# Two graph layers with residual norms on one core: when the norm steps of a pair enter the instruction streams

## The chip, the cores and the metric

The kernel runs on one core of a Trainium2 chip. The core's engines work side by side, each through its own stream of instructions in a fixed order: TensorE (PE in the profile) multiplies matrices and writes to PSUM, VectorE (DVE) and ScalarE (ACT) do elementwise work and read PSUM out, GpSimd (POOL) does elementwise work on SBUF, and SyncE (SP) issues the transfers. Engines wait for each other by semaphores. The metric is the device time of one execution in microseconds, the median of several; lower is better.

## The reference

There are 64 graphs of 256 nodes with 512 features. Two layers follow each other, each with a residual and a layer norm:

```python
# layer 0
deg = sum(adj, axis=-1)
agg = (adj @ x) / max(deg, 1e-6)
x1  = layernorm(x + relu(concat([x, agg]) @ W.T))
# layer 1
q, k = split(x1 @ Wqk);  v = x1 @ Wv
agg  = adj @ (k * mask)
w    = mask * (q . agg) / sqrt(512)          # one score per node
out  = layernorm(x1 + softmax(w, over nodes) * v)
```

All is fp32. The kernel forms `Wq Wk^T` once, so that layer 1 needs one product of x1 for the scores, one for the values and one with adj.

## The kernel before

Graphs are handled in 32 pairs. Every large product is a block product of the Strassen kind: seven products P1 to P7 of sums of blocks instead of eight. P1, P2, P3 and P5 are split a second time by `inner`, P4, P6 and P7 are done by `outer`, and products with adj by `gather`. The sums of blocks are made ahead by VectorE and GpSimd.

`inner` works with a bank `w` and a pair of banks `q`. Each unit ends in copies by ScalarE that the next unit of the same product, or the next product on the same bank, must wait for:

```python
def inner(p, X, sides, w, q, done=lambda fifth: None):
    ...
    def first_two():
        mm(hi, s(0), b["T1"], start=True)
        mm(lo, X.chunk(block, 0, 0), b["B11"])
        act.copy(q[0][:, :HF], lo)
        tick()
    def second():
        mm(lo, s(1), b["T2"])
        act.copy(q[0][:, HF:], lo)
        tick()
    def third():
        mm(lo, s(2), b["T3"])
        act.copy(q[1]..., lo[...])                 # 512 columns
        act.copy(fifth[0], hi)
        mm(q[0][:, :HF], X.chunk(block, 0, 1), b["B21"])
        tick()
    def last_two():
        mm(q[1][:, :HF], X.chunk(block, 1, 1), b["T4"])
        mm(q[0][:, HF:], s(3), b["B22"])
        if p in ("P1", "P5"):
            for k in range(2):
                vec.tensor_add(q[k][:, HF:], q[k][:, HF:], fifth[0])
        done(fifth[0])                             # copies or adds the product out
        tick()
```

The program is written out by `run`, whose string names the order of the units; `run("i k i k", ...)` takes a unit of i, one of k, and so on. Work that belongs to no product (norms, softmax, masks, degrees) stands in `chains` and is taken step by step by `tick`, after a unit, when a clock kept while the program is built says that the step's engine would be free. `room` is how far ahead of that clock an engine may be booked (0.6 us; -9.0 lets it take nothing), and `flush` takes all steps of a chain at once:

```python
def tick():
    while not quiet[0]:
        for c in list(chains):
            if c[2][0] <= clock[0] and c[3][0][0].free <= clock[0] + room[c[3][0][0]]:
                step(c)
                break
        else:
            return

def hasten(name, left):
    for c in list(chains):
        if c[1] == name and len(c[3]) == left:
            step(c)
            step(c)
```

A norm of one graph (two tiles of 128 nodes, NT = 2) is this chain; its last scaling opens a further chain with the two transposes of the tiles (`turn`), and after those of both graphs 16 transfers place the transposed x1:

```python
return [(vec, mean)] + [(act, lambda t=t: square(t)) for t in range(n)] + [(act, factor), (vec, shifts)] + [
    (act, lambda t=t: scale(t)) for t in range(n)]
```

In the profile `square` is `junk<-own,less`, `factor` is `rstd`, `shifts` is `shift<-less,rstd`, and `scale` is `own<-own,shift,rstd`. `adj<-adj,mask_sb` are the masks of adj for layer 1.

The main loop, with the parts concerned (j is the pair; layer 0 of pair j is interleaved with layer 1 of pair j - 1):

```python
i = inner("P1", X, W0, pw[0], u, a1)
k = inner("P5", X, W0, pw[1], y, a5)
m = inner("P2", X, W0, pw[0], o, a2)
...
elif j == 1:
    early.append(a1)
    run("k i k m k i k", i=early[0], k=k, m=m)
    fourth_sums(X, [1])
    run("m p p", m=m, p=p)
...
else:                                     # j > 1
    run("i k", i=i, k=k)
    send_scores(j - 2)
    run("i l k", i=i, k=k, l=open1)
    flush("norm")
    ...
...
if j == 1:
    turn_here(Y, owns[0], 0, pw)          # transposes by TensorE, for the first pair
    flush("mask")
    sumsM[0] = adj_sums(0)
    load_rows(2)
    run("s", s=s)
    turn_here(Y, owns[0], 1, pw)
    inner_sums(Y, gp, 0)
    ...
# end of layer 1 of pair j - 1; p is its P4, open1 its P3
b8()
run("p l p l", p=p, l=open1)
if j < NP - 1:
    hasten("norm", NT + 1)
run("p l", p=p, l=open1)
```

Of the kernel before, what the change touches and what calls it, by code (L numbers as in the profile page):

```python
# [94 lines left out]
def resnorm_kernel(  # L95
# [15 lines left out]
    NT, NF, NA = N // P, F // P, A // P  # L111
    H, HF = NF // 2, F // 2
    NP = B // 2
# [21 lines left out]
    room = {vec: 0.6, act: 0.6}  # L135
# [8 lines left out]
    def step(chain):  # L144
        _, name, ready, steps = chain
        eng, work = steps.popleft()
        work()
        ready[0] = eng.free + (0.4 if eng is not vec else 0.7 if name == "norm" and len(steps) == NT else 2.2 if name == "finish" or name == "norm" and steady else 1.4) if steps and steps[0][0] is not eng else 0.0
        if not steps:
            chains.remove(chain)  # L150
# [10 lines left out]
    def flush(*names):  # L161
        while True:
# [1 line left out]
            if not c:  # L164
                return
            step(c)

    def hasten(name, left):

        for c in list(chains):  # L170
            if c[1] == name and len(c[3]) == left:
                step(c)
                step(c)

    def run(order, **units):
        for name in order.split():
            units[name].pop(0)()
# [454 lines left out]
    def turn_here(X, x1, k, ps):  # L632

        for t in range(NT):
            for c in range(NF):
                tc.keep_in_program_order(nc.tensor.matmul(
                    ps[t][:, c * P:(c + 1) * P], x1[:, k, t, c * P:(c + 1) * P], ident, is_transpose=True,
                    start=(c == 0), stop=True, skip_group_check=True))
            act.copy(X.a[:, k, :, :, t].rearrange("p h e m -> p (h e) m"), ps[t].rearrange("p (c m) -> p c m", c=NF))
# [123 lines left out]
    pu, py, pf, pw = banks  # L763
# [3 lines left out]
    for j in range(NP):  # L767
        X = Xs.pop(j)
        if j == 2:
            steady.append(True)  # L770
        flush("finish")
        owns[j] = pool.tile([P, 2, NT, F], F32, name="own", bufs=3)
        if j > 0:
            load_adj(j)
            run_now(late_sums)
            late_sums.clear()
            sumsA[j] = adj_sums(j)

        u, y, o = pf, py, pu
        ys[j] = pool.tile([P, 2, NT, F], F32, name="y")  # L780
        a1, a2, a3, a4, a5, a6, a7 = layer0(j, o, u, y)
# [3 lines that stand above are left out]
        p, q = pairs(u, X, S2, W0["T2"], a6), pairs(u, X, S3, W0["T3"], a7)  # L785
        r, s = inner("P3", X, W0, pw[1], y, a3), pairs(u, X, A22, W0["T4"], a4)
        if j == 0:
            run("i k i k i k i k", i=i, k=k)
            flush("degrees")
            load_rows(1)  # L790
        elif j == 1:
            early.append(a1)
            run("k i k m k i k", i=early[0], k=k, m=m)
            fourth_sums(X, [1])
            run("m p p", m=m, p=p)
            fourth_sums(X, [0])
            run("p p m", m=m, p=p)
            load_x(1)
# [5 lines that stand above are left out]
            fetch_scores(j - 2)  # L804
            places[0](range(16))
            run("i k i k", i=i, k=k)
        if j != 1:
            fourth_sums(X, [1])
        if j > 1:
            flush("mask")  # L810
            sumsM[j - 1] = adj_sums(j - 1)
            if j + 1 < NP:
                load_rows(j + 1)
            load_x(j)
        if j > 1:
            softmax(j - 2)
            shared[0] = 1.0
        if j != 1:
            run("m p p", m=m, p=p)
            fourth_sums(X, [0])  # L820
            run("m p p m", m=m, p=p)
        flush("w0a")
        run("q q q", q=q)
        flush("w0")
        run("r q r m", m=m, q=q, r=r)
        if j == 1:
            flush("norm")
        quiet[0] = j < 2
        room[vec] = -9.0 if j > 1 else 0.6
        run("r s r", r=r, s=s)  # L830
        if j > 0:
            Y = x1Ts.pop(j - 1)
        if j > 1:
            inner_sums(Y, gp, 0)
            queue(1, "sums", *outer_sums(Y, vec), (vec, lambda Y=Y: inner_sums(Y, gp, 1)))
        T_late = []
        T = sums_T(ys[j], T_late, 0 if j < 2 else 1)

        if j == 0:
            degrees(1)  # L840
        zs[j] = pool.tile([P, 2, NT, HF], F32, name="z")
        g = gather(sumsA.pop(j), T, zs[j], pw[1], y[1], y[0], owns[j], rdegs[j], T_late)

        def sums_next():
            if j == NP - 1:
                return
            inner_sums(Xs[j + 1], gp, 0)
            rest = outer_sums(Xs[j + 1], gp)
            run_now(rest[:1])
            inner_sums(Xs[j + 1], gp, 1)  # L850
            late_sums.extend(rest[1:])
        if j == 0:
            sums_next()
            held = [c for c in chains if c[1] == "w1"]
            chains[:] = [c for c in chains if c[1] != "w1"]
            early.append(inner("P1", Xs[1], W0, pw[0], u, lambda fifth: early[1](fifth)))
            run("s s a b s c d i e i g f", s=s, i=early[0], **g)
            quiet[0] = False
        else:
            u2, o2, y2 = o, pf, y  # L860
            b1, b2, b3, b4, b5, b6, b7, b8 = layer1(j - 1, ys[j][:, :, 0], o2, u2, y2)
            jj = inner("P1", Y, W1, pw[0], u2)
            k = inner("P2", Y, W1, y[0], o2, b2)
            if j == 1:
                turn_here(Y, owns[0], 0, pw)
                flush("mask")
                sumsM[0] = adj_sums(0)
                load_rows(2)
                run("s", s=s)
                turn_here(Y, owns[0], 1, pw)  # L870
                inner_sums(Y, gp, 0)
                sums_Y = (*outer_sums(Y, vec), (vec, lambda: inner_sums(Y, gp, 1)))
                run("s a b s d c", s=s, **g)
                quiet[0] = False
                flush("w1")
                run("e j g f", j=jj, **g)
                queue(1, "sums", *sums_Y)
                run("k j k j k j", j=jj, k=k)
                b1(None)
                run("k", k=k)  # L880
            else:
                run("s s j s a b", s=s, j=jj, k=k, **g)
                room[vec] = 0.6
                run("j", j=jj)
                if j < NP - 1:
                    degrees(j + 1)
                run("c d j k e j", s=s, j=jj, k=k, **g)
                quiet[0] = True
                run("k", k=k)
                quiet[0] = False  # L890
                b1(None)
                run("g f", **g)
        flush("softmax", "adds", "sums", "degrees")
        if j > 0:
            aggs[j - 1] = late.tile([P, 2 * N_SIDE], F32, name="agg").rearrange(
                "p (k t f) -> p k t f", k=2, t=NT)
            vs[j - 1] = [late.tile([P, NT, F], F32, name="v", bufs=2) for _ in range(2)]
            T = sums_T(owns[j - 1])
            g = gather(sumsM.pop(j - 1), T, aggs[j - 1], pw[0], o2[1], o2[0])
            h, q = pairs(u2, Y, S2, W1["T2"], b6), pairs(u2, Y, S3, W1["T3"], b7)  # L900
            n = inner("P5", Y, W1, pw[1], y2, b5)
            p, open1 = pairs(u2, Y, A22, W1["T4"], b4), inner("P3", Y, W1, pw[1], y2, b3)
            norm0(j)
            mask_adj(j)
            run("k h h" if j > 1 else "h h", k=k, h=h)
            if j == 1:
                degrees(2)
                flush("degrees")
            if j < NP - 1:
                load_xT(j + 1)  # L910
            run("n k h h" if j > 1 else "n h h", k=k, n=n, h=h)
            fourth_sums(Y)
            shared[0] = 1.25
            sums_next()
            run("a n b q d q n c q e q n p g f", n=n, q=q, p=p, **g)
            b8()
            run("p l p l", p=p, l=open1)
            if j < NP - 1:
                hasten("norm", NT + 1)
            run("p l", p=p, l=open1)  # L920
            py, pu = pu, py
        else:
            norm0(0)
            mask_adj(0)
            chains.extend(held)
# [113 lines left out]
```

## Time and profile before

| | before |
|---|---|
| median of 3 runs | 1907.98 us (1907.01 to 1908.05) |
| span of the profiled execution | 1906.3 us |
| TensorE, matmuls | 1862.3 us, 98% |
| VectorE | 1502.3 us, 79% |
| ScalarE | 1309.5 us, 69% |
| GpSimd | 905.4 us, 47% |
| granted TensorE clock | 0.998 |
| mean DMA rate | 95 GB/s |

A line of the timeline gives the start in us from the span's beginning, the length, the engine, the operation with the tile written and the tiles read, the shape, how many neighbours were merged (x2), and in brackets how long the engine had been idle and whose work ended that. `bank` is a PSUM bank. Matmul lengths are modelled and overlap, so the distance of two starts says more than a length. A line of the waits gives who waited for whom, the total in us, how often, and the longest. Pairs j = 2 to 31 repeat one pattern every 58.2 us; the first pair and the second have orders of their own.

### The profile page before, as it was taken

The page shows a single profiled execution, that of the slowest core. Times are in us where ns is not written, and L with a number is a line of the kernel's source. Part 1 is how long each engine was busy: PE and PEld are TensorE (multiplying, and loading weights), DVE is VectorE, ACT ScalarE, POOL GpSimd, SP SyncE. Part 2 cuts the span into 40 slices and gives each one's busy share as a digit, 9 for nine tenths or more (in the row PEclk, how much of TensorE's full clock was granted, in tenths as well). Part 3 has the DMA queues.
Part 4 walks back from the last instruction along what each step waited for, and adds up shares of the span by engine and source line. Part 5 has one row for each costly group of instructions (what it writes and reads, how often), then busy time and mean ns, then how long its engine had stood idle before and what let it go on. Part 6 is the DMA issues. An engine that isn't in the chain of part 4 may idle for free.

```text
span 1906.3 us, 24928 instructions
## 1 busy us (share of the span) xinstructions
PE 1862.3 (98%) x7002; PEld 1318.2 (69%) x7002; DVE 1502.3 (79%) x3180; ACT 1309.5 (69%) x3274; POOL 905.4 (47%) x1255
## 2 busy tenths in 40 slices
PE   9999999999999999999999999999999999999997
PEld 5666767767676667677677766676776776766765
DVE  7787887777878778777778777787777787777877
ACT  3667776677776677766777766777667677667766
POOL 5455443455443554544554435545345544355532
PEclk9999999999999999999999999999999999999999
DMA  6133344342343333333423433334434233333321
GB/s 222 56 73 84 96 109 106 73 110 79 100 106 93 96 84 97 109 106 73 107 82 100 106 96 94 84 97 109 106 73 115 76 99 105 101 89 84 98 63 51
DMA packets 380714, 181.26 MB, mean 95 GB/s; under 512 B 263713, under 2 KB 345249, under 8 KB 380577
## 3 DMA queue, kind: packets, MB, share of 16 engines
q1 hardware_dynamic: 380576, 179.67, 34.8%
q8 instruction: 57, 0.93, 0.2%
q14 instruction: 81, 0.66, 0.1%
HBM read 114.10 MB, written 34.06 MB: 78 GB/s over the span
## 4 chain that ended last, share of the span: by engine, by line
PE 79%; DVE 8%; ACT 7%; issue 4%; POOL 1%; POOLq 0%; DVEq 0%; ACTq 0%
PE bank L182 79%; DVE v L90 3%; ACT own L90 3%; DVE bank L90 2%; ACT bank L90 1%; ACT junk L90 1%; DVE y L90 1%; DVE agg L90 1%; ACT y L90 1%; POOL xT_i L90 1%; DVE own L90 1%; ACT fifth L90 1%; DVE shift L90 0%; POOL xT_s L90 0%; POOL sa L90 0%
## 5 line engine op out<-in xcount | busy, mean ns | idle before, releaser
L90 ACT COPY bank<-bank 128x256 f32<-128x256 f32 (+1 forms) x768 | 333.8, 435 | 293.5 <-PE bank L182 280.3
L90 DVE TENSOR_TENSOR y<-bank,y 128x512 f32<-128x512 f32 x256 | 170.8, 688 | 149.4 <-ACT y L90 115.3
L90 POOL TENSOR_TENSOR x1T_i<-x1T_s 128x128 f32<-128x128 f32 x128 | 101.9, 796 | 216.4 <-DVE x1T_s L90 216.4
L90 ACT ACTIVATE own<-own,shift,rstd 128x512 f32<-128x512 f32 x255 | 197.2, 811 | 5.8 <-DVE shift L90 4.3
L182 PE MATMUL bank<-tv,sa 128*128 128x256 f32 x768 | 192.5, 380 | 0.9 <-DVE tv L90 0.9
L90 POOL TENSOR_TENSOR x1T_s<-x1T,x1T_s 128x256 f32<-128x256 f32 x64 | 63.8, 1017 | 270.3 <-PE bank L182 270.3
L90 ACT ACTIVATE junk<-own,less 128x512 bf16<-128x512 f32 x254 | 182.9, 720 | 3.0 <-DVE less L90 2.0
L182 PEld LDWEIGHTS bank<-tv,sa 128*128 128x128 f32 x768 | 145.4, 190 | 49.6 <-issue 22.9
L90 ACT COPY y<-bank 128x512 f32<-128x512 f32 x192 | 109.1, 585 | 98.7 <-PE bank L182 96.3
L182 PE MATMUL bank<-w,x1T_s 128*128 128x512 f32 (+1 forms) x384 | 168.3, 521 | 0.0
L182 PE MATMUL bank<-t_i,xT_i 128*128 128x256 f32 x512 | 155.0, 384 | 12.9 <-ACT fifth L90 12.6
L90 DVE TENSOR_TENSOR v<-bank,v 128x512 f32<-128x512 f32 x186 | 119.4, 683 | 53.7 <-PE bank L182 53.7
L182 PE MATMUL bank<-t,xT_s 128*128 128x512 f32 (+1 forms) x384 | 158.3, 521 | 0.8 <-ACT own L90 0.8
L182 PE MATMUL bank<-t,x1T_s 128*128 128x512 f32 (+1 forms) x384 | 158.1, 521 | 0.3 <-ACT y L90 0.3
L182 PE MATMUL bank<-w,xT_s 128*128 128x512 f32 (+1 forms) x384 | 153.1, 521 | 0.0
L182 PE MATMUL bank<-t_i,x1T_i 128*128 128x256 f32 x512 | 152.2, 379 | 0.1
L90 POOL TENSOR_TENSOR x1T_i<-x1T 128x256 f32<-128x256 f32 x64 | 53.2, 831 | 201.8 <-DMA x1T<-turn 189.0
L182 PEld LDWEIGHTS bank<-t_i,xT_i 128*128 128x128 f32 x512 | 94.1, 189 | 78.4 <-issue 45.5
L182 PEld LDWEIGHTS bank<-t_i,x1T_i 128*128 128x128 f32 x512 | 97.1, 190 | 67.1 <-issue 50.9
L90 POOL TENSOR_TENSOR xT_s<-xT,xT_s 128x256 f32<-128x256 f32 x62 | 45.1, 729 | 187.4 <-PE bank L182 187.4
L182 PE MATMUL bank<-t,x1T 128*128 128x512 f32 x256 | 130.6, 592 | 0.0
L182 PE MATMUL bank<-w,xT_i 128*128 128x256 f32 x384 | 116.5, 385 | 14.1 <-ACT bank L90 14.1
(159 smaller groups left out, 4562.5 us busy)
## 6 DMA issues: line engine op xcount, KB each, us to landing
x<-x SPq DMA_DIRECT2D x64, 512.0 KB, 5.8
xT<-x_t SPq DMA_DIRECT2D x62, 512.0 KB, 5.7
out<-own SPq DMA_DIRECT2D x62, 512.0 KB, 3.6
x1T<-turn SPq DMA_DIRECT2D x480, 64.0 KB, 2.3
adj<-adj_t SPq DMA_DIRECT2D x64, 256.0 KB, 2.9
turn<-adj SPq DMA_DIRECT2D x64, 256.0 KB, 3.1
row<-d SPq DMA_DIRECT2D x31, 256.0 KB, 4.7
wqk<-wqk_t SPq DMA_DIRECT2D x4, 512.0 KB, 5.9
```

Of the source, the lines that this page charges most:

```text
L90: return self.tc.keep_in_program_order(getattr(self.engine, name)(out, *args, **kwargs))
L182: tc.keep_in_program_order(nc.tensor.matmul(ps, a, b, start=start, stop=True, skip_group_check=True))
```

## The change

Three places. First, the call of `hasten` and the function are gone: before the last P4 and P3 units of a pair, the norm chain of its second graph (the one with NT + 1 = 3 steps left) no longer has its `shifts` and first `scale` put in ahead of time; they are taken by `tick` or by the later `flush("norm")`. Second, in the second pair (j = 1) VectorE takes no queued step while the units up to P1's last one are written out, so that the additions at the end of P1 stand first in its stream. Third, in the same pair the masks of adj and GpSimd's sums of the masked adj come behind both sets of copies of the transposed x1, and GpSimd's first sums of x1 come ahead of them.

```diff
-    def hasten(name, left):
-
-        for c in list(chains):
-            if c[1] == name and len(c[3]) == left:
-                step(c)
-                step(c)
...
         elif j == 1:
             early.append(a1)
-            run("k i k m k i k", i=early[0], k=k, m=m)
+            run("k i k", i=early[0], k=k)
+            room[vec] = -9.0
+            run("m k i k", i=early[0], k=k, m=m)
+            room[vec] = 0.6
             fourth_sums(X, [1])
...
             if j == 1:
                 turn_here(Y, owns[0], 0, pw)
+                run("s", s=s)
+                turn_here(Y, owns[0], 1, pw)
                 flush("mask")
+                inner_sums(Y, gp, 0)
                 sumsM[0] = adj_sums(0)
                 load_rows(2)
-                run("s", s=s)
-                turn_here(Y, owns[0], 1, pw)
-                inner_sums(Y, gp, 0)
                 sums_Y = (*outer_sums(Y, vec), (vec, lambda: inner_sums(Y, gp, 1)))
...
-            run("p l p l", p=p, l=open1)
-            if j < NP - 1:
-                hasten("norm", NT + 1)
-            run("p l", p=p, l=open1)
+            run("p l p l p l", p=p, l=open1)
```

## Prediction, before the run

> **What bounds the kernel now.** I read four views of the kernel before in this order: the busy shares, TensorE's waits, the timelines of TensorE and ScalarE over one pair in the middle, and the timelines of the second pair (50 to 100 us).
>
> ```profile
> PE 1862.3 (98%) x7002; PEld 1318.2 (69%) x7002; DVE 1502.3 (79%) x3180; ACT 1309.5 (69%) x3274; POOL 905.4 (47%) x1255
> PEclk9999999999999999999999999999999999999999
> ```
>
> TensorE (PE) is busy for 98% of the span at full clock, so only what makes TensorE stand still can be won. Its waits, by what ended them, for the whole kernel:
>
> ```profile
> PE bank L182 <- ACT bank L90: 14.1, 31, 0.5
> PE bank L182 <- ACT fifth L90: 12.6, 30, 0.7
> PE bank L182 <- DVE ones L90: 1.2, 1, 1.2
> ```
>
> Two waits come about once per pair of graphs (30 and 31 times), both on ScalarE (ACT) copies out of PSUM; nothing else reaches 1.3 us. Where they lie in one pair (start, length, instruction, idle before it):
>
> ```profile
> 288.15 0.59 PE L182 MATMUL bank<-w,xT 128*128 128x256 f32 x2
> 289.22 0.67 PE L182 MATMUL bank<-t_i,xT_i 128*128 128x256 f32 x2 [0.47 <-ACT fifth L90]
> ...
> 306.09 0.59 PE L182 MATMUL bank<-w,xT_i 128*128 128x256 f32 x2
> 307.14 0.67 PE L182 MATMUL bank<-w,xT_i 128*128 128x256 f32 x2 [0.46 <-ACT bank L90]
> ```
>
> The idle figure understates the loss, since matmuls are pipelined. Two such matmuls start 0.43 us after the two before them elsewhere in this timeline, so the ones at 289.22 were due at 288.58 (0.64 late), and the next ones follow at 289.72, after 0.50 instead of 0.43. One stall costs 0.71 us; the other, due at 306.52 and started at 307.14, costs 0.62 + 0.08 = 0.70. A second count agrees. From the counts of the groups over 32 pairs, a pair has 168 matmuls of 256 columns, spaced 0.2155 us (0.43 for two), and 48 of 512 columns, spaced 0.43: 36.2 + 20.6 = 56.84 us. Pairs repeat every 58.24 us (the dot products on VectorE at 285.06 and 343.30). The difference, 1.40 us, is the two stalls and nothing more.
>
> What ScalarE does before each:
>
> ```profile
> 286.20 0.36 ACT L90 COPY bank<-bank 128x256 f32<-128x256 f32 x1 [0.93 <-PE bank L182]
> 286.77 1.52 ACT L90 ACTIVATE own<-own,shift,rstd 128x512 f32<-128x512 f32 x2 [0.22 <-DVE shift L90]
> 288.20 0.57 ACT L90 COPY bank<-bank 128x512 f32<-128x512 f32 x1
> 288.71 0.36 ACT L90 COPY fifth<-bank 128x256 f32<-128x256 f32 x1
> ...
> 305.42 0.59 ACT L90 COPY y<-bank 128x512 f32<-128x512 f32 x1 [0.50 <-PE bank L182]
> 305.91 0.72 ACT L90 ACTIVATE junk<-own,less 128x512 bf16<-128x512 f32 x1
> 306.53 0.19 ACT L90 ACTIVATION_READ_ACCUMULATOR junk<-own,less 128x1 f32 x1
> 306.62 0.37 ACT L90 COPY bank<-bank 128x256 f32<-128x256 f32 x1
> ```
>
> The first stall is the two scalings that the helper hasten forces in at the pair's end: the last P3 copies, ready about 287.49 (their matmuls start at 286.85 and take 0.59), sit behind them until 288.20, and the next P5 needs that bank. The second is a squaring (junk) in front of the copy that frees a bank for P3's third unit.
>
> **What the skill says.** The Trainium skill, "Perfetto Trace Analysis", section Identifying Dependency Chains, says to find the gaps on the engine that binds and what ends each; the waits above do that. The same page, section Per-engine timelines, says that ScalarE and VectorE are strict FIFOs and that TensorE's end is an estimate. The trace agrees: the copy ready at 287.49 stays behind the scalings until 288.20, and busy PE time per pair (57.34 us) is above the 56.84 us of the spacing. "PSUM — Partial Sum Buffer", section PSUM bank collisions, asks for a semaphore between engines on one bank; here a matmul started 0.15 us after the fifth copy's end (289.07 to 289.22). I use that hand-over below.
>
> **The change, part by part.** The instruction order of both programs is fixed when they are built, so it can be compared beforehand. TensorE's order is the same in both, no arithmetic is added, and ScalarE, VectorE and GpSimd only change order.
>
> *Removing hasten, first stall, 30 pairs.* The order is now: P3 copy, fifth, first P1 copy, first P5 copy, scaling, second P1 copy, scaling, second P5 copy. On ScalarE a 256-column copy holds the engine for 0.28 us, a 512-column one for 0.5, a scaling for 0.715 (starts of neighbours above). P3's copies end at 287.49 + 0.88 = 288.37; with 0.15 the bank is free at 288.52, before 288.58: the stall goes. But the scalings now stand between P1's and P5's copies. The first runs about 289.92 to 290.64; the second P1 copy then ends at 291.01, just in time for P1's third unit (291.16). The second scaling pushes the second P5 copy to 291.62 to 291.98; with 0.15 this is 0.11 after P5's third unit is due (292.02), plus 0.07 of restart. Behind it, VectorE now makes two transposes instead of one (0.63 each) before the last addition of P1, so the copy of P1 lets P6 start about 0.1 late, partly the same delay. I leave 0.2 us: gain 0.71 - 0.20 = 0.51.
>
> *Second stall, 30 pairs.* With the build-time clock differently placed, the squaring moves behind the second P3 copy. That copy waits only for its matmuls, ending 0.55 to 0.6 earlier than now, and ends 0.08 before it is needed. Gain 0.70. The two squarings and scalings of the finished graphs move later: the last two scalings go into an idle stretch of ScalarE (1.56 us before the P3 copy at 343.17; they take 1.43), so nothing there should wait. Sum per pair 1.21; times 30 = 36.3 us.
>
> *The second pair.* Two parts, met once each.
>
> ```profile
> 58.05 1.42 DVE L90 TENSOR_TENSOR bank<-bank,fifth 128x256 f32<-128x256 f32 x4
> ...
> 59.24 3.67 PE L182 MATMUL bank<-t,xT_s 128*128 128x512 f32 x8 [0.82 <-ACT own L90]
> ...
> 74.08 1.32 ACT L90 ACTIVATE adj<-adj,mask_sb 128x256 f32<-128x256 f32 x3
> ...
> 76.90 1.99 PE L182 MATMUL bank<-y,adj 128*128 128x256 f32 x8 [0.78 <-ACT x1T L90]
> ```
>
> VectorE's additions at 58.05 stand behind four norm steps although the matmuls ended at 57.11; without those, P6 starts near 58.35 instead of 59.24: 0.9 won. The masks (1.32 us) leave the copies of the transposed x1: 0.8 won. Against these: the norm of the second graph slips. Its shift now stands behind P2's last additions on VectorE (about 71.2), and ScalarE then does two scalings (1.43) before the copy that P3's last unit needs, which starts near 73.5 instead of 71.62. Also six small preparations of the second weight (0.42 us each, 2.5 us) move to the two that already stand behind the sums for the gather, ahead of the VectorE addition at 83.34 that a gather product waits for. So after the two gains I put the first multiplication with adj 1.0 later, and the gather product another 2.3 later. Other small waits may shrink by 0.8. Net for this pair: 2.5 us lost.
>
> *Sum:* 1907.98 - 36.3 + 2.5 = 1874.2; I round down to 1873, since the losses in the second pair rest on one long chain of guesses.
>
> **The rivals.**
> (1) *The stalls turn into new ones.* The scalings still need 1.43 us of ScalarE in a row of PSUM copies with margins of 0 to 0.1 us. For it: the computed margins are that thin. Against it: ScalarE idles for 0.9 to 1.0 us twice just there (before 290.36 and 292.08). If 0.5 us comes back per pair, the gain is 0.9 x 30 = 27 and the time 1883.
> (2) *Everything goes.* If the margins hold, 1.40 x 30 = 42 us are won; with a neutral second pair 1866.
> (3) *VectorE or the transfer of the transposed x1 becomes the bound.* The last two transposes come later, and TensorE arrives about 1.3 us sooner at the first product with x1T. Against it: GpSimd starts on x1T at 307.91 and has its first result at 308.63, and TensorE needs it at 311.52, 2.9 us later; transposes end within 0.2 us of where they do now. It should leave 1.6 us spare and cost nothing.
> (4) *The removed help was needed*: finished outputs leave later (the second near 343 instead of 327.54). They block only the next transfer of adj, whose sums are wanted much later than they are ready. It should cost nothing.
>
> **Range and chances.** The 30 steady pairs decide: each 0.1 us per pair is 3 us. Residual stalls between 0.05 and 0.45 us, and a second pair between a gain of 1.5 and a loss of 4, give 1864 to 1884. The 2% mark is 1869.8, a total gain of 38.2 us: nearly all of both stalls must go and the second pair must not lose. I give that 0.30; slower by 2% would need a new stall over 2.6 us in each pair, 0.01.
>
> **What would show it.** In TensorE's waits, the 0.7 us waits on fifth should vanish, and the 31 waits on bank fall to short ones or move to the third unit of P5; a pair should take 57.0 to 57.1 us instead of 58.24. ScalarE should show one scaling after the first P5 copy and one after the second P1 copy, and the squaring behind the second P3 copy. In the second pair, P6 should start near 58.4, P3's last unit near 73.5, and the VectorE addition now at 83.34 should come after a block of eight weight preparations. I am wrong if a pair still takes over 57.4 us (rival 1), or if the second pair ends earlier than now.

## The result, and the profile after

| | before | after |
|---|---|---|
| median of the timed runs | 1908.01 us (1907.01 to 1908.45) | 1883.89 us (1882.62 to 1885.35) |
| after / before, 95% interval | | 0.9875 [0.9857, 0.9892] |
| span of the profiled execution | 1906.3 us | 1880.8 us |
| mean of 29 pairs, from one softmax reduction (`top<-row` on VectorE) to the next | 58.21 us | 57.26 us |

The change saves 24 us, where 35 were predicted. The page of the kernel after (busy time, share of the span, instructions; then the granted clock) shows a TensorE that is still the bound:

```profile
PE 1858.1 (99%) x7002; PEld 1313.6 (70%) x7002; DVE 1512.2 (80%) x3180; ACT 1309.1 (70%) x3274; POOL 909.5 (48%) x1255
PEclk9999999999999999999999999999999999999999
```

TensorE's waits after (who waited for whom, us in total, times, longest):

```profile
PE bank L175 <- ACT bank L90: 2.3, 2, 2.0
PE bank L175 <- DVE z L90: 2.2, 1, 2.2
PE bank L175 <- POOL sa L90: 1.9, 9, 0.3
```

Both stalls that came once a pair are gone: no wait on `fifth` is left, and the 31 waits on `bank` are down to two. In their place stand two long waits met once (2.0 and 2.2 us) and, unexpectedly, nine short ones put down to GpSimd's `sa`. One of them (0.20 us at 51.74) stood in the kernel before too; the other eight come at the start of P6, which does not read `sa`.

**One pair of the steady part.** ScalarE (start, length, instruction, idle before it):

```profile
289.88 0.36 ACT L90 COPY bank<-bank 128x256 f32<-128x256 f32 x1 [0.51 <-PE bank L175]
290.14 0.81 ACT L90 ACTIVATE own<-own,shift,rstd 128x512 f32<-128x512 f32 x1
290.86 0.37 ACT L90 COPY bank<-bank 128x256 f32<-128x256 f32 x1
291.16 0.81 ACT L90 ACTIVATE own<-own,shift,rstd 128x512 f32<-128x512 f32 x1
291.88 0.85 ACT L90 COPY bank<-bank 128x256 f32<-128x256 f32 x2
...
305.62 0.38 ACT L90 COPY bank<-bank 128x256 f32<-128x256 f32 x1
305.92 0.72 ACT L90 ACTIVATE junk<-own,less 128x512 bf16<-128x512 f32 x1
```

and TensorE in the same stretch:

```profile
291.40 0.59 PE L175 MATMUL bank<-w,xT_i 128*128 128x256 f32 x2
291.83 0.60 PE L175 MATMUL bank<-w,xT 128*128 128x256 f32 x2
292.39 0.67 PE L175 MATMUL bank<-t,xT_i 128*128 128x256 f32 x2
292.89 0.59 PE L175 MATMUL bank<-t,xT_s 128*128 128x256 f32 x2
```

The two scalings stand singly between copies, the squaring stands behind P3's second copy. What remains is P5's third unit: 0.56 after its neighbour instead of 0.43, and the next ones 0.50 later instead of 0.43. That is 0.13 + 0.07 = 0.20 us.

**Two kinds of pairs.** Pairs do not all take the same time. Of the 29, thirteen take 57.33 to 57.67 us, thirteen 56.77 to 57.14, and three lie between. VectorE in a long pair of the kernel after:

```profile
634.44 0.69 DVE L90 TENSOR_TENSOR v<-bank,v 128x512 f32<-128x512 f32 x1 [1.61 <-PE bank L175]
635.24 0.96 DVE L90 TENSOR_TENSOR v<-v,fifth 128x256 f32<-128x256 f32 x1
636.12 0.68 DVE L90 TENSOR_TENSOR v<-bank,v 128x512 f32<-128x512 f32 x1
636.83 0.43 DVE L90 TENSOR_TENSOR v<-v,fifth 128x256 f32<-128x256 f32 x1
637.17 1.30 DVE L90 STREAM_TRANSPOSE turn<-own 128x512 f32<-128x512 f32 x2
638.39 1.39 DVE L90 TENSOR_TENSOR bank<-bank,fifth 128x256 f32<-128x256 f32 x4
```

GpSimd beside it:

```profile
633.00 0.73 POOL L90 TENSOR_TENSOR sa<-adj 128x256 f32<-128x256 f32 x1 [4.93 <-DMA adj<-adj_t]
633.81 0.73 POOL L90 TENSOR_TENSOR sa<-sa,adj 128x256 f32<-128x256 f32 x1
634.50 0.73 POOL L90 TENSOR_TENSOR sa<-adj 128x256 f32<-128x256 f32 x1
635.19 0.72 POOL L90 TENSOR_TENSOR sa<-adj,sa 128x256 f32<-128x256 f32 x1
```

and TensorE, at the start of P6:

```profile
638.75 0.60 PE L175 MATMUL bank<-w,xT 128*128 128x256 f32 x2
639.55 1.96 PE L175 MATMUL bank<-t,xT_s 128*128 128x512 f32 x4 [0.21 <-POOL sa L90]
```

The first addition of `v` takes 0.96 us; its twin 1.6 us later takes 0.43. In nine of the 29 pairs the first takes 0.81 us or more, and all nine are long ones; in two more of the long ones it is the second addition (0.92 us each). All that follows on VectorE without idle time (the transposes, then P1's additions) moves by the difference, and P6, which waits for the copy of P1 to `own`, starts 0.80 after its neighbour instead of 0.43. The wait is put down to GpSimd, but what P6 lacked was this copy on ScalarE, whose first half starts at 638.82 and ends at 639.41:

```profile
638.82 1.07 ACT L90 COPY own<-bank 128x512 f32<-128x512 f32 x2 [1.60 <-DVE bank L90]
```

In a short pair VectorE's addition started first:

```profile
291.97 0.42 DVE L90 TENSOR_TENSOR v<-v,fifth 128x256 f32<-128x256 f32 x1
```

and GpSimd's sum was the one that took longer:

```profile
292.02 0.96 POOL L90 TENSOR_TENSOR sa<-adj,sa 128x256 f32<-128x256 f32 x1
```

Before the change these sums started some 10.3 us ahead of the softmax reduction that closes the stretch (635.43 for the one at 645.71); after it, 6.7 us ahead (633.00 for 639.69), beside the additions of `v`. The first sum and the first of the two additions before the change:

```profile
635.43 0.72 POOL L90 TENSOR_TENSOR sa<-adj 128x256 f32<-128x256 f32 x1 [1.39 <-DMA adj<-adj_t]
641.88 0.43 DVE L90 TENSOR_TENSOR v<-v,fifth 128x256 f32<-128x256 f32 x1
```

The sums wait for adj: GpSimd's wait for that transfer grew from 40.9 us in 30 waits to

```profile
POOL sa L90 <- DMA adj<-adj_t: 153.6, 30, 6.7
```

The queue of SyncE shows why. Before:

```profile
327.54 0.38 SPq L187 DMA_DIRECT2D out<-own  x1
340.58 0.88 SPq L187 DMA_DIRECT2D adj<-adj_t  x2
```

After:

```profile
342.06 0.38 SPq L180 DMA_DIRECT2D out<-own  x1
342.55 1.34 SPq L180 DMA_DIRECT2D adj<-adj_t  x2
```

The second graph's output used to be gone 13 us before adj was due. Without the helper it is finished only around 342 us, and stands in SyncE's fixed order ahead of adj, which can go only behind it: 13.9 us ahead of the pair's softmax reduction before the change (354.50), 10.8 us after it (353.39).

**The second pair.** TensorE after, with what it waited for:

```profile
58.39 1.96 PE L175 MATMUL bank<-t,xT_s 128*128 128x512 f32 x4
...
72.93 0.70 PE L175 MATMUL bank<-t_i,xT_s 128*128 128x256 f32 x2 [2.00 <-ACT bank L90]
...
87.62 1.13 PE L175 MATMUL bank<-y,sa 128*128 128x256 f32 x4 [2.19 <-DVE z L90]
```

P6 starts on time (58.39), and the waits of 0.82 and 0.78 us of before are gone. In their place P3's last unit waits 2.00 us, behind two scalings whose shift came late, and a gather product waits 2.19 us. ScalarE ahead of P3's last unit (the copy that it needs starts at 72.31):

```profile
70.88 1.52 ACT L90 ACTIVATE own<-own,shift,rstd 128x512 f32<-128x512 f32 x2 [1.60 <-DVE shift L90]
```

VectorE ahead of the gather product:

```profile
83.43 0.94 DVE L90 TENSOR_TENSOR t_i<-w 128x256 f32<-128x256 f32 x1
...
86.88 0.68 DVE L90 TENSOR_TENSOR z<-bank,z 128x512 f32<-128x512 f32 x1
```

Eight weight preparations stand in front of the addition to `z` that TensorE waits for. From the pair's first product of P1 (51.77 before, 51.74 after) to the first softmax reduction (121.44 and 124.38; the expectations of two runs below call it the first dot products), the second pair takes 69.67 us before and 72.64 after: 3.0 us lost.

### The profile page after: what moved, and what is told of

Its sections match the earlier page's. It is cut to its first block, busy times and chain, and to the rows that moved or that the text cites. A ratio compares the mean times of both kernels' runs of the same rounds, so it can differ in the third digit from the quotient of the medians.

```text
span 1880.8 us, 25016 instructions
## 1 busy us (share of the span) xinstructions
PE 1858.1 (99%) x7002; PEld 1313.6 (70%) x7002; DVE 1512.2 (80%) x3180; ACT 1309.1 (70%) x3274; POOL 909.5 (48%) x1255
## 4 chain that ended last, share of the span: by engine, by line
PE 94%; POOL 2%; DVE 2%; issue 2%; ACT 1%; POOLq 0%; ACTq 0%; DVEq 0%
PE bank L175 94%; POOL xT_i L90 1%; POOL xT_s L90 1%; POOL sa L90 0%; ACT own L90 0%; DVE own L90 0%; DVE v L90 0%; PE bank L629 0%; DVE tv L90 0%; DVE t_i L90 0%; ACT bank L90 0%; DVE turn L90 0%; DVE w L90 0%; DVE bank L90 0%; DVE st L90 0%
## 5 line engine op out<-in xcount | busy, mean ns | idle before, releaser
L90 POOL TENSOR_TENSOR sa<-adj 128x256 f32<-128x256 f32 x128 | 94.4, 738 | 153.6 <-DMA adj<-adj_t 153.6
L175 PEld LDWEIGHTS bank<-t_i,xT_i 128*128 128x128 f32 x512 | 94.6, 190 | 58.4 <-issue 46.4
L90 ACT COPY own<-bank 128x512 f32<-128x512 f32 x128 | 71.9, 587 | 91.1 <-PE bank L175 49.6
```

The lines of the kernel that those rows point to most:

```text
L90: return self.tc.keep_in_program_order(getattr(self.engine, name)(out, *args, **kwargs))
L175: tc.keep_in_program_order(nc.tensor.matmul(ps, a, b, start=start, stop=True, skip_group_check=True))
```

## The experiments

Two figures carry the comparisons: the mean of the 29 steady pairs, and the length of the second pair as just defined.

| kernel | time, us | ratio to before | mean pair, us | second pair, us |
|---|---|---|---|---|
| before | 1908.0 | 1 | 58.21 | 69.67 |
| after | 1883.89 | 0.9875 [0.9857, 0.9892] | 57.26 | 72.64 |
| helper removed only | 1879.95 | 0.9860 [0.9844, 0.9877] | 57.23 | 69.33 |
| helper removed, masks moved | 1878.57 (one run) | | 57.25 | 68.89 |
| helper removed, stretch | 1883.44 | 0.9873 [0.9857, 0.9890] | 57.26 | 72.50 |
| squaring moved only | 1887.73 | 0.9893 [0.9879, 0.9906] | 57.53 | |
| after, adj sent first | 1878.97 | 0.9855 [0.9840, 0.9869] | 57.06 | |
| after, sums of adj later | 1878.91 | 0.9854 [0.9840, 0.9869] | 57.07 | |
| no stretch, adj first | 1873.03 | 0.9816 [0.9803, 0.9830] | 57.06 | 69.09 |
| the same, a scaling earlier | 1870.74 | 0.9804 [0.9791, 0.9818] | 56.98 | 68.74 |

The rows come from several chips, and the kernel before took 1906.80 to 1908.20 us beside them. Each ratio is to the kernel before on the same chip, so ratios compare better than times.

The second pair is left out for the squaring alone, which changes nothing there, and for two runs in whose profiles the granted clock of TensorE stood at 0.50 for 3.4 us of it: with adj sent first once (from 88.7 us), with the sums of adj later twice (from 73.2 and from 90.2 us). They took 74.23 and 75.60 us there, 1.6 and 3.0 us more than the kernel after, so their profiled spans understate their gain over it. A second profile of the kernel after has one such fall (from 74.3 us; 74.18 us for the pair). Three kernels with the same order in the second pair itself (no stretch, masks moved) give 68.74 to 69.09, so differences under 0.4 us in that column mean little.

### Which part of the change does what

The kernel before with only the helper removed:

```diff
-            run("p l p l", p=p, l=open1)
-            if j < NP - 1:
-                hasten("norm", NT + 1)
-            run("p l", p=p, l=open1)
+            run("p l p l p l", p=p, l=open1)
```

> The kernel before with only the helper at the pair's end taken away; the second pair has the orders of before. By the profile, the first softmax reduction comes at 121.44 us before and at 124.38 in the changed kernel. Theory (the second pair's new orders cost 2.9 us, the helper has no part in it): it comes at 121.4 again, and the time is 1881, 2.9 below the changed kernel. Rival (the loss comes in over the pairs, not in the second): 124.4 and 1884.

It took 1879.95 us, 26.9 us less than the kernel before beside it (1906.80), where the whole change gained 24.1. It has steady pairs like those of the kernel after (57.23 and 57.26) and a second pair like that of the kernel before. So the gain is the helper's removal alone. The kernel after without the stretch in which VectorE takes no step:

```diff
-            run("k i k", i=early[0], k=k)
-            room[vec] = -9.0
-            run("m k i k", i=early[0], k=k, m=m)
-            room[vec] = 0.6
+            run("k i k m k i k", i=early[0], k=k, m=m)
```

> The changed kernel without the stretch in which VectorE takes no queued step: the helper is gone and the masks stand behind the copies of the transposed x1. Theory (the masks' move wins 0.8 us, the VectorE stretch loses 3.7): the first softmax reduction comes at 120.6 us and the time is about 1880. Rival (the masks' move is what loses): 124 or later.

Its second pair takes 68.89 us: 3.75 less than after, and 0.44 less than with the helper's removal alone, which is about the scatter of that figure. The counterpart is the kernel after with the masks back in front of the copies:

```diff
                 turn_here(Y, owns[0], 0, pw)
-                run("s", s=s)
-                turn_here(Y, owns[0], 1, pw)
                 flush("mask")
-                inner_sums(Y, gp, 0)
                 sumsM[0] = adj_sums(0)
                 load_rows(2)
+                run("s", s=s)
+                turn_here(Y, owns[0], 1, pw)
+                inner_sums(Y, gp, 0)
```

> The changed kernel with the masks of adj in the second pair back where they stood before (ahead of the copies of the transposed x1), so that of the second pair's two parts only the stretch without norm steps on VectorE is left. From the second pair's first product of pair 1 to the first dot products the runs so far took 69.7 us in the kernel before, 72.6 in the changed one and 68.9 with the masks alone. If the parts add, this one takes 72.6 + 0.4 = 73.1 us or up to 73.4, and the time is 1884 to 1886. If the loss came from the two parts together (masks and late scalings on one ScalarE), it takes under 71 us and the time is about 1882.

72.50 us instead of the 73.1 to 73.4 that a sum of the parts would give, and a time equal to that of the whole change. So the stretch loses about 3 us by itself (72.50 against 69.33), and beside it the masks' move is worth nothing: TensorE's wait on P3's last unit is 2.91 us here and 2.00 in the kernel after, the wait on the gather product 0.78 and 2.19. What one wait gives back the other takes.

The stretch may have a further cost. Of the five profiles of kernels with it, three have the falls of the clock to 0.50 named above, each behind one of TensorE's two long waits (2.0 and 2.2 us); of the six profiles of kernels without it, none has one in this part. No run shows why the clock fell, and two profiles with such waits lack it.

### The two stalls, one by one

The kernel before with its helper, but with ScalarE kept from taking a squaring ahead of P3's second copy (one of the squarings of each pair moves, then the small steps behind it):

```diff
-            run("r q r m", m=m, q=q, r=r)
+            run("r", r=r)
+            if j > 1:
+                room[act] = -9.0
+            run("q", q=q)
+            if j > 1:
+                room[act] = 0.3
+            run("r m", m=m, r=r)
+            room[act] = 0.6
```

> The kernel before with one thing changed: ScalarE may not take a squaring between the y copy and P3's second copy, and takes one of the two behind that copy and one behind the third. The helper that forces the scalings stays, and so do the orders of all other engines and the second pair. My theory: the two stalls are independent, so the 30 waits on bank fall away and the 30 waits on fifth (0.7 us each) stay; a pair falls from 58.2 to 57.5 us (0.70 less), and the time to 1887 (30 x 0.70 = 21 less), about 0.989. Rival: the second stall followed from the first (the arrival of TensorE behind the first stall decides it), and taking the squaring away frees under 0.3 us per pair: time above 1899.

A pair takes 57.53 us, 0.68 less than before, and the time is 1887.73 us. TensorE's waits in this kernel:

```profile
PE bank L182 <- ACT fifth L90: 12.7, 30, 0.6
...
PE bank L182 <- ACT bank L90: 0.3, 1, 0.3
```

The second stall is gone and the first one is where it was. They are independent, and the sizes of the prediction (0.70 and, for the first, 0.71 less what remains) hold: 57.53 to 57.06, the undisturbed pair without the helper, is 0.47 for the first.

### Where the rest of the gain went

Two theories. One: adj comes too late, and something waits for it. The other: adj is early enough for TensorE, but its sums now run beside VectorE's additions and hold those up. First the transfer: the kernel after with the next adj sent ahead of the second output, so that only SyncE's order differs.

```diff
+        if j == 1:
+            load_adj(j)
         if j > 0:
-            load_adj(j)
             run_now(late_sums)
...
             b8()
+            if j < NP - 1:
+                load_adj(j + 1)
             run("p l p l p l", p=p, l=open1)
```

> The changed kernel, with the transfer of the next pair's adj put ahead of the second finished output in SyncE's queue; every other engine's order is that of the changed kernel. Theory (the late output holds the adj transfer back, GpSimd's sums of adj then run beside VectorE's last additions of the pair and slow them): every pair takes 57.05 to 57.1 us, GpSimd's wait for adj falls from 153.6 to about 40 us in all, and the time is 1877 to 1879, some 6 us below the changed kernel. Rival (VectorE is late by its own two transposes, whatever GpSimd does): half of the pairs still take 57.35 to 57.57 and the time stays at 1884.

1878.97 us, a mean of 57.06 us (from one first addition of `v` to the next, all but the last of the 29 take 57.05 or 57.06), and GpSimd waits for adj as little as before (40.7 us in 30 waits). This shows that the order of output and adj is the cause, but both theories allow it. So the other: adj as late as in the kernel after, but GpSimd's sums of it moved behind sums of x for a later product.

```diff
-            sumsA[j] = adj_sums(j)
+            if j == 1:
+                sumsA[j] = adj_sums(j)
...
             fourth_sums(X, [0])
+            if j > 1:
+                sumsA[j] = adj_sums(j)
             run("m p p m", m=m, p=p)
```

> The changed kernel, with GpSimd's first sums of adj put some 8 us later in GpSimd's order (behind its sums for P3); the adj transfer stays late. If the collision of GpSimd's sums with VectorE's additions is what costs, pairs take 57.05 to 57.1 us and the time is about 1878, as with the early transfer. If it is the late transfer itself (its traffic, or the queue behind it), the long pairs stay and the time is 1884.

GpSimd in this kernel, in the pair whose softmax reduction on VectorE comes at 298 us:

```profile
285.68 1.29 POOL L90 TENSOR_TENSOR xT_s<-xT 128x512 f32<-128x512 f32 x1
297.08 0.73 POOL L90 TENSOR_TENSOR xT_s<-xT,xT_s 128x256 f32<-128x256 f32 x1 [10.11 <-PE bank L175]
297.76 0.73 POOL L90 TENSOR_TENSOR sa<-adj 128x256 f32<-128x256 f32 x1
```

GpSimd stands still for 10.11 us where the sums were, VectorE has the stretch for itself (its additions of `v` at 294.11 and 295.18 take 0.42 and 0.43 us), and the gain is the same to the tenth: 57.07 us a pair and 1878.91 us. The transfer is still behind the output (344.70 after 344.21 in SyncE's queue) and it costs nothing. The collision is the cause.

### A better version

The kernel after without the stretch and with adj first:

> The changed kernel without the stretch in which VectorE takes no step in the second pair, and with the transfer of the next adj issued ahead of the second output. From the runs so far: 120.4 us up to the first dot products (masks moved, no stretch), 29 pairs of 57.06 us = 1654.8, and 96 us behind them: a span of 1871.2 and a time of 1873, or 1875 if a stretch at a lower granted clock falls into the first 100 us as it did in two earlier profiles; about 0.982. If the loss by the stretch in the second pair and the loss by the late adj were not additive, the time would stay at 1877 or more.

1873.03 us, 57.06 us a pair and 69.09 for the second: the two repairs add up. Run again beside it on the same chip, the kernel after took 1885.37 us (1884.21 to 1886.03).

> The changed kernel once more, beside the others on the same chip. 1883.9 us, as measured before; pairs of two kinds, 57.1 and 57.4 to 57.6 us.

Last, the 0.20 us left at P5's third unit. On top of the kernel just told, the first scaling goes ahead of the first P5 copy (`scale_one`, a new helper, takes the steps of the norm chain up to and with its next scaling):

```diff
-            run("i k", i=i, k=k)
+            run("i", i=i)
+            scale_one()
+            room[act] = -9.0
+            run("k", k=k)
             send_scores(j - 2)
-            run("i l k", i=i, k=k, l=open1)
+            run("i", i=i)
+            scale_one()
+            room[act] = 0.6
+            run("l k", k=k, l=open1)
```

> The kernel of the run before (no stretch, adj first), and in every pair from the third on the first of the second graph's two scalings goes ahead of the first P5 copy instead of behind it; the second stays behind the second P1 copy. One instruction moves per pair, on ScalarE alone. In the changed kernel P5's third unit is 0.2 us late behind the second P5 copy, which stands behind the second scaling. Theory: with the scalings at about 289.3 and 290.6 instead of 290.14 and 291.16 (times of the changed kernel) that copy starts when its matmuls are done, the 0.2 us goes, and a pair takes 56.86 to 56.95 us, since 56.84 is what the matmuls alone need: 29 x 0.15 to 0.2 = 4 to 6 us less, time 1867 to 1870. Rival: P6 then becomes late by the same amount, since VectorE's chain to P1's last additions does not move and its margin is 0.17 us; then a pair takes 57.0 us and the time stays within 2 us of the run before.

1870.74 us (1870.53 to 1871.12, beside 1872.75 to 1873.19 without it). A pair falls by 0.07 us, less than the theory gave, since its rival is half right. TensorE in this kernel, P5's third unit and the start of P6:

```profile
287.63 0.59 PE L182 MATMUL bank<-w,xT 128*128 128x256 f32 x2
288.07 0.59 PE L182 MATMUL bank<-t,xT_i 128*128 128x256 f32 x2
...
291.09 0.59 PE L182 MATMUL bank<-w,xT 128*128 128x256 f32 x2
291.56 1.96 PE L182 MATMUL bank<-t,xT_s 128*128 128x512 f32 x4
293.35 0.59 PE L182 MATMUL bank<-t_i,xT_i 128*128 128x256 f32 x2
```

P5's third unit comes 0.44 after its neighbour, on time. P6 is now 0.04 late, and what follows it another 0.07 (1.79 after P6's start for four matmuls of 0.43): 0.11 of the 0.20 came back where VectorE's chain sets the start. This is the fastest kernel of the study, 2.0% below before and 0.8% below the change run beside it (1885.37).

## Why the prediction was right and wrong

- **The two stalls: right.** Both vanish. The prediction left 0.20 us at P5's third unit, behind the second scaling, and 0.20 was found there. Where nothing else interferes a pair takes 57.06 us; 57.0 to 57.1 was predicted.
- **Late outputs and adj: the step that failed.** The prediction held under its fourth rival that the late outputs "block only the next transfer of adj, whose sums are wanted much later than they are ready. It should cost nothing." Every fact in it was right but the conclusion. The question asked was when TensorE needs the sums; the one not asked was which instruction of VectorE they would then run beside. VectorE's addition then took up to 0.98 us instead of 0.42, and P6 started late. The collision costs 0.20 us a pair in the mean (57.26 against 57.06), 5.6 us over 29 pairs. In the ratios 3.7 us of it show (the kernel with adj first gained 27.8 us, the change 24.1), and the low clock in the second pair may have taken back some of the rest.
- **Rival 1, right in size and wrong in cause.** It gave 1883 us for 0.5 us a pair returning through ScalarE's copies. The time agrees by chance; the copies returned only the 0.20 already counted, and the rest came through VectorE.
- **The second pair: right in kind, near in size and partly by luck.** 2.5 us of loss predicted, 3.0 found. The first product with adj came 0.55 us later (76.90 to 77.45) where 1.0 was predicted, the gather product 3.29 later (84.33 to 87.62) where 1.0 + 2.3 was. P6's start at 58.4 and the eight preparations ahead of the addition came as told; P3's last unit started at 72.93 instead of near 73.5. The 0.8 us given for the masks was the mis-sized term: with the stretch their move gains nothing, since TensorE waits further down anyway (72.50 us for the pair without the move, 72.64 with it). Since the sum counted on these 0.8 us, its agreement is in part luck.
- **Rival 3: right.** No wait of TensorE on the transposed x1 is among those after.
- **The sum.** The 10.9 us between 1873 and 1883.9: of 36.3 us predicted for the pairs, the 29 gained 27.7 and the last one 0.6, which leaves 8.0, namely 5.6 for the collision and 2.4 for pairs that gain slightly less than 1.21 us even without it; 0.4 for the second pair; 1.2 for rounding 1874.2 down to 1873; and 1.4 because the timed runs gained 24.1 us where the two profiled spans differ by 25.5 (the profiled execution of the kernel after was the fastest of its four, 1882.62 against a median of 1883.89). These make 11.0; the rest is rounding.

## What to carry to other kernels

When a step moves, follow what it releases through the in-order queues to the end, and ask of each instruction that shifts in time not only who waits for it but also whose neighbour it becomes. A work item with slack of many microseconds can still cost time if it lands beside an addition on the path that sets the end. A wait that ends with an engine that the matmul does not read from is a pointer to look at the chain behind it, and moving one suspect off the stretch while the other stays is the experiment that tells a late transfer from a collision.

## What the runs showed of the hardware

VectorE's addition of two SBUF tiles (128x256, fp32) took 0.42 us by itself and up to 0.98 us when a GpSimd addition on SBUF had started just before it; when VectorE started first, GpSimd's took 0.96 instead of 0.73. The Trainium skill, "SBUF — State Buffer", section Who interferes with whom, says that a VectorE instruction with two SBUF inputs contends with a GpSimd instruction that reads SBUF, that the one issued first has the shared ports for its whole length, and that the other waits. The trace agrees on the order, and shows how little decides: a start 0.05 us earlier or later (635.19 and 635.24 in the long pair, 292.02 and 291.97 in the short one) makes the difference of 0.4 us in the pair's time. The loss also falls with GpSimd's head start: where VectorE was slowed, head start and length add up to 1.00 or 1.01 us (0.05 + 0.96 at 635.24, 0.19 + 0.81 at 1493.52, 0.42 + 0.59 at 578.10). So VectorE's 0.42 us began some 0.58 us after GpSimd's start, somewhat sooner than the end of the 0.73 us that the profile gives GpSimd's addition. The addition at 634.44, with one input in PSUM, ran its usual 0.69 us beside a sum that started at 634.50.
